# A selective scan with a feed-forward layer on one core: C·h in two runs of four, and side work in six slots a half

## The chip, the cores and the metric

One core of a Trainium2 chip runs the whole program. The metric is the device time of one execution in microseconds. TensorE (PE) multiplies matrices into PSUM, which has eight banks here, all of them in use; ScalarE (ACT) and VectorE (DVE) read PSUM, GpSimd (POOL) works on SBUF alone, and SyncE (SP) issues the DMAs. Each engine runs its own instructions in the order in which the program emits them, and waits on semaphores for the others. The order is written by hand (`tc.manual_schedule()`): what the Python loop emits first stands first in each engine's queue.

## The reference

Two sequences of 1024 tokens with 512 channels go through a selective state-space layer, a residual and a layer norm, then a gated feed-forward layer (512 to 2048 and back), a residual and a layer norm. All values are fp32. The part that sets the shape of the kernel is the recurrence, with 128 states for each of 512 channels:

```python
def step(h, inp):
    dt, bt, ct, xt = inp
    h = jnp.exp(dt[:, :, None] * A) * h + (dt * xt)[:, :, None] * bt[:, None, :]
    y = jnp.einsum('bdn,bn->bd', h, ct)
    return (h, y)
```

`delta`, `B` and `C` come from projections of the normed and gated input; after the scan come `(y + x * D_param) @ out_proj_w.T` and `silu(x @ w_gate.T) * (x @ w_up.T) @ w_down.T`.

## The kernel before

**Rounds.** The 2048 tokens are 64 blocks (`st`) of 32 tokens. A block has two halves (`h`), a half eight rounds, so there are 1024 rounds `k`, and `r = k % 8` is the place of a round in its half. Each round scans 32 channels x 32 tokens for 128 states, as one row of 1024 elements. It emits, in this order:

- `work.others()`: one step of each piece of side work that is at a point marked "E" (ScalarE, GpSimd, VectorE or DMA work, among it what reads the bank of a finished side group).
- TensorE: two `bu` matmuls (L705, outer product of dt·x and B for this round, double-buffered banks), and two `a` matmuls (L417, dt·A of the **next** round). In the trace each fp32 matmul is two records, so a round has eight. The two `a` results have one bank each, so the next round's `a` can be written only when ScalarE has read this round's.
- ScalarE: in odd rounds of every block but the first of a sequence, L713 copies the state carried from the block before into the first column of `bu`; it stands ahead of the two `decay_exp` activations of the next round (L424, `a_sb`). In even rounds VectorE adds it (L723).
- VectorE: the scan (L726), which reads `a_sb` and `bu` and writes `h`.
- TensorE: the `y_round`s that `ROUNDS[r]` lists (L436, C·h of the half before, four matmuls for four tokens; eight `y_round`s a half), or up to four **parts** of side work.
- GpSimd: one `diag` (L388 or L398), which builds an operand for later `bu` or `a` matmuls.

**Side work.** The projections of the next tokens (`pre`), the output projection of finished tokens (`post`) and the feed-forward layer (`ffn`) are generators. They mark "P" before the first matmul of a group, "H" inside a group and "E" after its end. A part is what is emitted between two marks: two `gu` matmuls (L552), one `d` matmul (L574), one `op`, `sel` or `xp` matmul, two transposes. All side groups share one PSUM bank (`misc`, one buffer). A `gu`, `d` or `op` group has eight parts, `sel`, `xp` and `ss` four, the transposes two, `t0` one. `Work.tensor()` emits one part; once a group has ended it emits nothing more until the next `others()` has stepped the generator over its "E". So at most one group ends in a round, and its bank is read in the round after: by ScalarE (L560 for `gu`, L244, L256, L274/L275, L291, L314, L224/L228 for `pre`), or by VectorE (L580 for `d`, L474 for `zT`, L487 for `op`).

**How much a round takes** is set by a credit: each round adds `PARTS[r]`, the sum is cut to 6, and up to `min(credit, 4)` parts are emitted where `PARTS[r]` is not zero.

```python
ROUNDS = ((), (0, 1, 2), (), (), (3, 4, 5), (), (), (6, 7))
PARTS = (4, 0, 3, 3, 0, 3, 3, 0)
```

Both orders give 16 parts of credit a half, which is 128 for four blocks. The work for four blocks is 98 parts of `ffn`, 10 of `post` and some 19 of `pre`.

**After the loop** come the last eight `y_round`s, the last `post` and whatever side work is left, now with six banks and nothing between the groups.

Of the kernel before, what the change touches and what calls it, by code (L numbers as in the profile page):

```python
# [17 lines left out]
TC = 256  # L18


ROUNDS = ((), (0, 1, 2), (), (), (3, 4, 5), (), (), (6, 7))
PARTS = (4, 0, 3, 3, 0, 3, 3, 0)
RMS_EPS = 1e-6
LN_EPS = 1e-5

# [9 lines left out]
def kernel(  # L35
# [26 lines left out]
    NM = D // P  # L62
    NH = NF // 2
# [91 lines left out]

    made = {}

    def misc(name):
        return bank_pool[0].tile([P, 512], FP, tag="m", name=name)


# [3 lines left out]
    def pre(c):  # L165

        t0, n = lots[c]
        n_j, n_s = n // P, n // S
# [29 lines left out]
        for m in range(NM):  # L198
            nc.scalar.activation(xT[:, m, :], xT[:, m, :], AF.Copy, scale=col(V_NORM, m))
        yield "P"  # L200
        ps = misc(f"ss_{c}")
        for k in range(NM):
            nc.tensor.matmul(  # L203
                ps[:, 0:n], ones, u[:, k, :], start=(k == 0), stop=(k == NM - 1)
# [14 lines left out]


        for m in range(NM):
            ps = misc(f"sel_{c}_{m}")
            yield from matmuls(ps, sel_w, m, xn)
            nc.scalar.activation(  # L224
                u[:, m, :], ps[:, 0:n], AF.Relu,
                bias=neg[:, 1, m : m + 1], scale=neg[:, 0, m : m + 1],
            )
            nc.scalar.activation(  # L228
                dt[:, m, :], ps[:, 0:n], AF.Abs, bias=gate_b[:, m : m + 1], scale=col(V_GATE, m)
            )  # L230
            yield "P" if m + 1 < NM else "E"
# [7 lines left out]


        for g, dst in ((0, low), (2, c_sb)):
            ps = misc(f"xp_{c}_{g}")
            yield from matmuls(ps, xp_w, g, xn)
            nc.scalar.copy(dst, ps[:, 0:n])  # L244
            yield "P"

        ps = misc(f"b_{c}")
        for j in range(n_j):
            for k in range(NM):
                nc.tensor.matmul(  # L250
# [12 lines left out]
        yield "P"  # L263

        for a in range(0, NM, 2):
            ps = misc(f"z_{c}_{a}")
            for m in (a, a + 1):
                nc.tensor.matmul(  # L268
                    ps[:, ts(m - a, n)], dt_w[:, ts(m, P)], low, start=True, stop=True
                )  # L270
                yield "H" if m == a else "E"
            for m in (a, a + 1):
                z = ps[:, ts(m - a, n)]
                nc.scalar.activation(u[:, m, :], z, AF.Relu, bias=col(V_DTB, m))  # L274
                nc.scalar.activation(dt[:, m, :], z, AF.Abs, bias=col(V_DTB, m))  # L275
            yield "P" if a == 0 else "E"
# [4 lines left out]

        for j in range(n_j):
            yield "P"
            ps = misc(f"uT_{c}_{j}")
            for m in range(NM):
                nc.tensor.transpose(ps[:, ts(m, P)], u[:, m, ts(j, P)], ident)
                if m == 1:
                    yield "H"
            yield "E"
            t = pre_pool.tile([P, D], FP, tag="row", name=f"uT_{c}_{j}")  # L290
            nc.scalar.copy(  # L291
                t.rearrange("p (g m c) -> p m g c", g=4, m=NM),
                ps.rearrange("p (m g c) -> p m g c", m=NM, g=4),
            )
            for st in range(4):
                nc.sync.dma_start(  # L296
                    ub_d[t0 // S + 4 * j + st, :, :, 0, :].rearrange("g t q -> t g q"),
                    t[ts(st, S), :].rearrange("t (g q) -> t g q", g=4),
                )
            if c == 0:  # L300
                load(0)
                diag(0, 0)
                diag(0, 1)
        yield "P"
        ps = misc(f"t0_{c}")
        for m in range(NM):
            nc.tensor.matmul(
                ps[0:n_s, ts(m, P)],
# [149 lines left out]
    def post(tt):  # L458

        zT = post_pool.tile([P, NM, P], FP, tag="zT", name=f"zT_{tt}")  # L460
        nc.sync.dma_start(zT, x_q.rearrange("(m p) t -> p m t", p=P)[:, :, ts(tt, P)])
        yield "E"
        yield "E"
        nc.gpsimd.tensor_tensor(zT, zT, dq.unsqueeze(2).to_broadcast([P, NM, P]), ALU.mult)
        yield "E"
        yield "P"
        ps = misc(f"zT_{tt}")
        for s in range(4):
            nc.tensor.transpose(ps[:, ts(s, P)], yrs[tt][:, s, :], ident)
            if s == 1:  # L470
                yield "H"
        yield "E"
        z = zT.rearrange("p m (s t) -> p s m t", t=S)
        nc.vector.tensor_tensor(  # L474
            z, z, ps.rearrange("p (s m t) -> p s m t", m=NM, t=S), ALU.add
        )
        x1 = post_pool.tile([P, D], FP, tag="x1", name=f"x1_{tt}", bufs=4)
        nc.sync.dma_start(x1, xf[tt])
        yield "P"
        ps = misc(f"op_{tt}")  # L480
        for half in (slice(0, 256), slice(256, 512)):
            for k in range(NM):
                nc.tensor.matmul(  # L483
                    ps[:, half], zT[:, k, :], out_w[:, k, half], start=(k == 0), stop=(k == NM - 1)
                )
                yield "H" if half.start == 0 or k + 1 < NM else "E"
        nc.vector.tensor_tensor(x1, x1, ps, ALU.add)  # L487
        yield "E"
        yield from normalize(x1, f"a{tt}")
        work.add(ffn(tt, x1))  # L490

    def normalize(t, name):
# [10 lines left out]
    def ffn(tt, row):  # L503
# [4 lines left out]
        for what in order:  # L508
            part = int(what[1])
# [17 lines left out]
        fetch(4)  # L527
        x1T = ffn_pool.tile([P, NM, P], FP, tag="x1T", name=f"x1T_{tt}")
        yield "P"
        ps = misc(f"x1T_{tt}")  # L530
        for m in range(NM):
            nc.tensor.transpose(ps[:, ts(m, P)], row[:, ts(m, P)], ident)
            if m == 1:
# [4 lines left out]
        for what in order:  # L538
            part = int(what[1])
            if what[0] == "g":  # L540
                hid = hid_pool[0].tile([P, NH, P], FP, tag="hid", name=f"hid_{tt}_{part}")
                hids[part] = hid, []

                for f in range(0, NH, 2):
                    fetch(at + 4)
                    yield "P"
                    ps = misc(f"gu_{tt}_{part}_{f}")
                    for b in range(2):
                        w = pieces[at + b].rearrange("p (a k h) -> p a k h", a=2, k=NM)
                        for a in range(2):  # L550
                            for k in range(NM):
                                nc.tensor.matmul(  # L552
                                    ps[:, ts(2 * a + b, P)], w[:, a, k, :], x1T[:, k, :],
                                    start=(k == 0), stop=(k == NM - 1),
                                )
                                if k % 2:
                                    yield "E" if a and b and k + 1 == NM else "H"
                    at += 2
                    gu = ffn_pool.tile([P, 2, 2 * P], FP, tag="gu", name=f"gu_{tt}_{part}_{f}", bufs=2)
                    nc.scalar.copy(gu, ps.rearrange("p (a t) -> p a t", a=2))  # L560
                    work.add(
                        silu(gu, hid[:, f : f + 2, :], f"{tt}_{part}_{f}", hids[part][1]), front=True
                    )
                continue
            hid, ready = hids[part]
            while len(ready) < NH // 2:
                yield "E"
            for half in range(2):
                fetch(at + 4)
                yield "P"  # L570
                ps = misc(f"d_{tt}_{part}_{half}")
                for f in range(NH):
                    w = pieces[at + f // 4].rearrange("p (f d) -> p f d", f=4)
                    nc.tensor.matmul(  # L574
                        ps[:, 0:HD], hid[:, f, :], w[:, f % 4, :],
                        start=(f == 0), stop=(f == NH - 1),
                    )
                    yield "H" if f + 1 < NH else "E"
                part_of = row[:, ts(half, HD)]
                nc.vector.tensor_tensor(part_of, part_of, ps[:, 0:HD], ALU.add)  # L580
                at += 2
# [38 lines left out]
    class Work:  # L620


        def __init__(self):
            self.gens, self.holder = [], None

        def add(self, gen, front=False):
            item = [gen, next(gen)]
# [16 lines left out]
        def tensor(self):  # L644

            if self.holder is not None:
                if self.holder[1] != "H":
                    return False
                self.step(self.holder)
                return True  # L650
            for item in self.gens:
                if item[1] == "P":
                    self.holder = item
                    self.step(item)
                    return True
            return False

# [5 lines left out]
    work = Work()  # L663
# [16 lines left out]
    pres, begun, credit = {}, set(), 0  # L680
    for k in range(NG):
        h, m, pair = place(k)
        st, i = divmod(h, 2)
        r = k % 8
        work.others()
        if r == 0:
# [4 lines left out]
            if i == 0:  # L691
                c = lot_of[st]
# [10 lines left out]
        for b in range(2):  # L703
            g = 2 * pair + b
# [28 lines left out]
            for b in ROUNDS[r]:  # L733
                y_round(h - 1, b)
        credit = min(credit + PARTS[r], 6)
        for _ in range(min(credit, 4) if PARTS[r] else 0):
            if not work.tensor():
                break
            credit -= 1

        j, r4 = divmod(k, 4)
        if r4 == 3:
# [92 lines left out]
```

## Time and profile before

| what | us |
|---|---|
| median of three runs (2877.61 to 2884.94) | 2881.35 |
| the profiled execution's own time | 2885.05 |
| its span, first to last instruction | 2882.4 |
| of the span: lead-in, up to the first round's first `bu` | 40.2 |
| the 1024 rounds (first `bu` of the first to first `bu` of the last) | 2752.0 |
| the last round and what follows the loop | 90.2 |

The stretches are read off the timeline of TensorE. A row of the timeline is: start, duration, engine, line, operation, output<-inputs, count, and in brackets the idle time of the engine before it with what ended it. In the waits, the numbers are total, times and longest. PE rows overlap: their ends are modelled, so a round is best measured from the start of its first `bu` to the start of the next round's.

### The profile page before, as it was taken

To read this page: it belongs to the slowest core of one execution; us is meant where nothing else is said; L and a number is where in the kernel's file an instruction comes from. 1 tells how busy PE (TensorE), PEld (TensorE's weight loads), DVE (VectorE), ACT (ScalarE), POOL (GpSimd) and SP (SyncE) were. 2 spreads that over 40 slices of the span, in tenths; PEclk is the share of its full clock that TensorE was granted. 3 is DMA by queue.
4 is the path that set the end of the run, shared out by engine and by line. 5 is a ranking of instruction groups with operands and counts; after the bars stand their busy time and mean duration, and the time that the engine had idled before them with its cause. 6 is when DMAs were issued, how large, how long until landed. Compare 5 with 4: busy or idle time off the path is not lost.

```text
span 2882.4 us, 58142 instructions
## 1 busy us (share of the span) xinstructions
PE 2781.4 (96%) x22728; PEld 1518.3 (53%) x22728; DVE 2460.8 (85%) x1680; ACT 1640.0 (57%) x3663; POOL 1838.5 (64%) x2140
## 2 busy tenths in 40 slices
PE   7989899999999999999999999999999999999998
PEld 4434454555555555455555555555555555555558
DVE  3998789899998988898998988889998899889970
ACT  4656556555665556555666556655566555555543
POOL 4666576666666666666666666566666666666643
PEclk6999999999999999999999999999999999999999
DMA  2012221324223231223312332222331332333337
GB/s 75 20 34 74 88 89 63 96 73 136 82 76 105 89 122 52 85 96 103 105 56 82 114 103 100 67 91 83 118 100 55 111 100 96 112 102 107 103 107 234
DMA packets 139166, 266.86 MB, mean 93 GB/s; under 512 B 22480, under 2 KB 76240, under 8 KB 138896
## 3 DMA queue, kind: packets, MB, share of 16 engines
q1 hardware_dynamic: 138896, 263.16, 28.5%
q8 instruction: 182, 2.98, 0.4%
q14 instruction: 88, 0.72, 0.1%
HBM read 250.39 MB, written 12.71 MB: 91 GB/s over the span
## 4 chain that ended last, share of the span: by engine, by line
PE 84%; DVE 7%; issue 3%; ACT 3%; POOL 1%; DMA 1%; SPq 0%; DVEq 0%; ACTq 0%; POOLq 0%
PE bu L705 30%; PE gu L552 17%; PE y L436 15%; PE d L574 7%; PE a L417 7%; DVE h L726 6%; PE sel L186 2%; PE op L483 2%; PE xp L186 1%; ACT a_sb L424 1%; DMA ub_d<-uT 1%; PE b L250 1%; PE ss L203 0%; PE z L268 0%; SPq L296 0%
## 5 line engine op out<-in xcount | busy, mean ns | idle before, releaser
L726 DVE TENSOR_TENSOR_SCAN h<-a_sb,bu 128x1024 f32<-128x1024 f32 x1024 | 2326.7, 2283 | 267.1 <-ACT bu L713 144.4
L424 ACT ACTIVATE a_sb<-a 128x496 f32<-128x496 f32 x2048 | 1084.8, 582 | 445.5 <-PE a L417 370.1
L417 PE MATMUL a<-ddt,a_t 32*128 32x512 f32 x4096 | 1275.7, 647 | 7.5 <-ACT a_sb L424 4.7
L705 PE MATMUL bu<-du,ub 32*128 32x512 f32 x4096 | 1224.8, 646 | 28.1 <-DVE h L726 22.7
L388 POOL TENSOR_TENSOR ddt<-dt,hot 128x512 f32<-128x512 f32 x512 | 532.8, 1048 | 291.5 <-PE a L417 291.5
L552 PEld LDWEIGHTS gu<-x1T,w 128*128 128x128 f32 x4096 | 481.9, 192 | 231.1 <-issue 175.2
L398 POOL TENSOR_TENSOR du<-ub,hot 128x512 f32<-128x512 f32 x512 | 534.8, 1048 | 38.9 <-PE a L417 35.2
L552 PE MATMUL gu<-x1T,w 128*128 128x128 f32 x4096 | 536.8, 283 | 11.0 <-ACT x1T L536 3.5
L705 PEld LDWEIGHTS bu<-du,ub 32*128 32x128 f32 x4096 | 351.5, 184 | 354.3 <-issue 209.5
L436 PE MATMUL y<-h,cz 128*32 128x256 f32 x8192 | 523.3, 384 | 1.2 <-DVE h L726 1.2
L436 PEld LDWEIGHTS y<-h,cz 128*32 128x32 f32 x8192 | 227.3, 109 | 403.2 <-issue 291.0
L713 ACT COPY bu<-cu 128x32 f32<-128x32 f32 x496 | 94.1, 190 | 578.0 <-PE a L417 514.5
L417 PEld LDWEIGHTS a<-ddt,a_t 32*128 32x128 f32 x4096 | 393.0, 185 | 47.7 <-ACT a_sb L424 28.8
L592 POOL TENSOR_SCALAR gu<-gu 128x256 f32<-128x256 f32 x128 | 108.2, 845 | 294.0 <-ACT gu L560 289.6
L574 PE MATMUL d<-w,hid 128*128 128x256 f32 x1024 | 257.1, 393 | 7.9 <-ACT t L314 3.0
L574 PEld LDWEIGHTS d<-w,hid 128*128 128x128 f32 x1024 | 184.2, 190 | 126.9 <-issue 81.6
L450 POOL TENSOR_TENSOR yc<-yc,pick 128x512 f32<-128x512 f32 x64 | 66.5, 1039 | 153.7 <-ACT yc L449 153.7
L723 DVE TENSOR_TENSOR bu<-bu,cd 128x32 f32<-128x32 f32 x496 | 92.9, 187 | 74.0 <-PE a L417 69.1
L600 POOL TENSOR_TENSOR hid<-gu,e 128x256 f32<-128x256 f32 x128 | 93.1, 728 | 65.5 <-ACT e L598 64.7
L374 POOL TENSOR_TENSOR cd<-cd,h 128x256 f32<-128x256 f32 x124 | 106.3, 857 | 39.9 <-DVE h L726 39.9
L560 ACT COPY gu<-gu 128x512 f32<-128x512 f32 x128 | 75.0, 586 | 60.3 <-PE gu L552 60.1
L593 POOL TENSOR_TENSOR gu<-gu 128x256 f32<-128x256 f32 x128 | 94.2, 736 | 10.7
(89 smaller groups left out, 1384.0 us busy)
## 6 DMA issues: line engine op xcount, KB each, us to landing
w<-in_wgu_s_dram SPq DMA_DIRECT2D x256, 512.0 KB, 4.8
w<-in_wd_s_dram SPq DMA_DIRECT2D x128, 512.0 KB, 3.8
cd<-dt_d SPq DMA_DIRECT2D x62, 256.0 KB, 3.4
ub<-ub_d SPq DMA_DIRECT2D x64, 128.0 KB, 2.0
cu<-ub_d SPq DMA_DIRECT2D x124, 64.0 KB, 4.8
ub_d<-bt SPq DMA_DIRECT2D x64, 64.0 KB, 1.7
ub_d<-uT SPq DMA_DIRECT2D x64, 64.0 KB, 1.8
zT<-in_x_q_dram SPq DMA_DIRECT2D x16, 256.0 KB
```

The lines of the kernel that those rows point to most:

```text
L374: nc.gpsimd.tensor_tensor(cd, cd, last, ALU.mult)
L388: nc.gpsimd.tensor_tensor(ddts[j][:, m, :, :], made[lot_of[st]][0][:, a + m, toks(st)].unsqueeze(1).to_broadcast([P, 16, S]), hot[:, ts(i, ...
L398: nc.gpsimd.tensor_tensor(dus[j][:, m, :, :], uv[:, a + m, :].unsqueeze(2).to_broadcast([P, 16, S]), hot.unsqueeze(1).to_broadcast([P, 16, ...
L417: nc.tensor.matmul(ps, a_t[ts(g, 32), m, :], ddts[k // 4][ts(g, 32), m % 2, :, :], start=True, stop=True,)
L424: nc.scalar.activation(a_sb[:, k % 3, ts(b, 16), 1:], ps[:, :, 1:], AF.Exp, scale=-1.0)
L436: nc.tensor.matmul(ys[st][ts(m, 32), ts(i, 256)], cz[st % 3][:, at : at + 32], hs[h][:, ts(m, 64), ts(b, 4)], start=(i == 0 and b == 0), s ...
L552: nc.tensor.matmul(ps[:, ts(2 * a + b, P)], w[:, a, k, :], x1T[:, k, :], start=(k == 0), stop=(k == NM - 1),)
L574: nc.tensor.matmul(ps[:, 0:HD], hid[:, f, :], w[:, f % 4, :], start=(f == 0), stop=(f == NH - 1),)
L592: nc.gpsimd.tensor_scalar_max(g, g, -80.0)
L593: nc.gpsimd.tensor_tensor(gu[:, 1, :], g, gu[:, 1, :], ALU.mult)
L705: nc.tensor.matmul(bu[:, ts(b, 16), :], prepared[st][ts(g, 32), 1, :], dus[k // 4][ts(g, 32), m % 2, :, :], start=True, stop=True,)
L726: nc.vector.tensor_tensor_scan(hs[h][:, ts(r, 32), :].rearrange("p q t -> p (q t)"), a_sb[:, k % 3, :, :].rearrange("p q t -> p (q t)"), b ...
```

## The change

The eight `y_round`s of a half go into two rounds (four in `r = 1`, four in `r = 5`) instead of three, and the parts into six rounds instead of five: 3, 2, 3, 3, 2, 3 in `r = 0, 2, 3, 4, 6, 7` (before 4, 3, 3, 3, 3 in `r = 0, 2, 3, 5, 6`). Each side group now tells `Work` how many parts it has, and the loop uses that for its last parts: a group with one part left is finished beyond the credit (up to four parts a round), and a round with three parts emitted and two left in the group stops. The instructions are the same in kind and number; their order changes.

```diff
-ROUNDS = ((), (0, 1, 2), (), (), (3, 4, 5), (), (), (6, 7))
-PARTS = (4, 0, 3, 3, 0, 3, 3, 0)
+ROUNDS = ((), (0, 1, 2, 3), (), (), (), (4, 5, 6, 7), (), ())
+PARTS = (3, 0, 2, 3, 3, 0, 2, 3)
...
-    def misc(name):
+    def misc(name, parts):
+        work.left = parts
         return bank_pool[0].tile([P, 512], FP, tag="m", name=name)
...
-                    ps = misc(f"gu_{tt}_{part}_{f}")
+                    ps = misc(f"gu_{tt}_{part}_{f}", 8)
...
-                ps = misc(f"d_{tt}_{part}_{half}")
+                ps = misc(f"d_{tt}_{part}_{half}", NH)
...
             if self.holder is not None:
                 if self.holder[1] != "H":
                     return False
+                self.left -= 1
                 self.step(self.holder)
                 return True
             for item in self.gens:
                 if item[1] == "P":
                     self.holder = item
                     self.step(item)
+                    self.left -= 1
                     return True
             return False
...
         credit = min(credit + PARTS[r], 6)
-        for _ in range(min(credit, 4) if PARTS[r] else 0):
+        done, most = 0, min(credit, 4)
+        while PARTS[r] and (done < most or done < 4 and work.left == 1):
+
+            if done == 3 and work.left == 2:
+                break
             if not work.tensor():
                 break
-            credit -= 1
+            done += 1
+        credit -= done
```

The other calls of `misc` get the sizes named above (`ss`, `sel`, `xp`: 4; `b`: one or two; `z`, `uT`, `zT`, `x1T`: 2; `t0`: 1; `op`: 8).

More of the change, by code (lines that the diff above doesn't have):

```diff
@@ L200, in pre @@
         yield "P"
-        ps = misc(f"ss_{c}")
+        ps = misc(f"ss_{c}", NM)
         for k in range(NM):
@@ L221, in pre @@
         for m in range(NM):
-            ps = misc(f"sel_{c}_{m}")
+            ps = misc(f"sel_{c}_{m}", NM)
             yield from matmuls(ps, sel_w, m, xn)
@@ L241, in pre @@
         for g, dst in ((0, low), (2, c_sb)):
-            ps = misc(f"xp_{c}_{g}")
+            ps = misc(f"xp_{c}_{g}", NM)
             yield from matmuls(ps, xp_w, g, xn)
@@ L245, in pre @@
             yield "P"
-        ps = misc(f"b_{c}")
+        ps = misc(f"b_{c}", n_j)
         for j in range(n_j):
@@ L265, in pre @@
         for a in range(0, NM, 2):
-            ps = misc(f"z_{c}_{a}")
+            ps = misc(f"z_{c}_{a}", 2)
             for m in (a, a + 1):
@@ L283, in pre @@
             yield "P"
-            ps = misc(f"uT_{c}_{j}")
+            ps = misc(f"uT_{c}_{j}", 2)
             for m in range(NM):
@@ L304, in pre @@
         yield "P"
-        ps = misc(f"t0_{c}")
+        ps = misc(f"t0_{c}", 1)
         for m in range(NM):
@@ L466, in post @@
         yield "P"
-        ps = misc(f"zT_{tt}")
+        ps = misc(f"zT_{tt}", 2)
         for s in range(4):
@@ L479, in post @@
         yield "P"
-        ps = misc(f"op_{tt}")
+        ps = misc(f"op_{tt}", 8)
         for half in (slice(0, 256), slice(256, 512)):
@@ L529, in ffn @@
         yield "P"
-        ps = misc(f"x1T_{tt}")
+        ps = misc(f"x1T_{tt}", 2)
         for m in range(NM):
@@ L623, in __init__ @@
         def __init__(self):
-            self.gens, self.holder = [], None
+            self.gens, self.holder, self.left = [], None, 0
         def add(self, gen, front=False):
```

## The prediction

> **What bounds the kernel now.** I read the page first: which engine the chain lies on, and the clock.
>
> ```profile
> span 2882.4 us, 58142 instructions
> ...
> PE 2781.4 (96%) x22728; PEld 1518.3 (53%) x22728; DVE 2460.8 (85%) x1680; ACT 1640.0 (57%) x3663; POOL 1838.5 (64%) x2140
> ...
> PEclk6999999999999999999999999999999999999999
> ...
> PE 84%; DVE 7%; issue 3%; ACT 3%; POOL 1%; DMA 1%; SPq 0%; DVEq 0%; ACTq 0%; POOLq 0%
> ```
>
> TensorE carries the chain at full clock. But 96% busy hides stalls, since PE rows overlap. So, second, the PE timeline of half a `gu` phase (rounds `r` = 5, 6, 7, 0):
>
> ```profile
> 977.43 0.69 PE L705 MATMUL bu<-du,ub 32*128 32x512 f32 x1
> ...
> 978.50 1.60 PE L552 MATMUL gu<-x1T,w 128*128 128x128 f32 x12
> 980.04 0.69 PE L705 MATMUL bu<-du,ub 32*128 32x512 f32 x1
> ...
> 981.11 0.71 PE L552 MATMUL gu<-x1T,w 128*128 128x128 f32 x4
> 981.75 0.69 PE L705 MATMUL bu<-du,ub 32*128 32x512 f32 x1
> ...
> 983.40 1.07 PE L436 MATMUL y<-h,cz 128*32 128x256 f32 x16
> 984.40 0.69 PE L705 MATMUL bu<-du,ub 32*128 32x512 f32 x1
> ```
>
> A round is measured from its first `bu` to the next. Three parts (12 records): 980.04 - 977.43 = 2.61. One part: 1.71. Undisturbed, the side group starts 1.07 after `bu`; in the round at 981.75 it starts 1.65 after it. That 0.58 is a stall inside the core matmuls, and the busy row doesn't show it. Over all rounds the medians are: 1, 2, 3, 4 parts of `gu` 1.71, 2.16, 2.61, 3.05 (`d`: 3.00 for four); two and three `y_round`s 2.07 and 2.50. So a part costs 0.44, a `y_round` 0.43, and opening a group 0.27 (parts) or 0.21 (`y`) above a bare 1.0. Summed over the timeline, starts later than 1.07 make 181 us.
>
> Third, what the stall waits for, in ScalarE's timeline:
>
> ```profile
> 983.14 0.19 ACT L713 COPY bu<-cu 128x32 f32<-128x32 f32 x1 [0.36 <-PE bu L705]
> 983.26 1.06 ACT L424 ACTIVATE a_sb<-a 128x496 f32<-128x496 f32 x2
> ```
>
> In an undisturbed round the two exps begin 1.24 after `bu` (even rounds) or behind L713 (odd), and end 2.26 or 2.46 after it. The next round's `a` matmuls wait for their banks. So a round shorter than 2.46 (odd) or 2.26 (even) makes the next one stall for the difference: 0.38 after two `y_round`s in `r = 7`, 0.75 after an odd one-part round. VectorE's floor is 4.67 for two rounds, back to back.
>
> Fourth, the waits for the shared side bank where VectorE drains it, and the stretch behind the loop:
>
> ```profile
> PEld d L574 <- DVE x L580: 10.0, 10, 1.4
> ...
> PEld op L483 <- DVE zT L474: 13.9, 11, 1.6
> ```
>
> ```profile
> 2795.93 3.64 PE L436 MATMUL y<-h,cz 128*32 128x256 f32 x58 [1.18 <-DVE h L726]
> 2799.50 3.72 PE L574 MATMUL d<-w,hid 128*128 128x256 f32 x16
> ...
> 2833.51 28.85 PE L552 MATMUL gu<-x1T,w 128*128 128x128 f32 x256 [2.06 <-ACT x1T L536]
> ...
> 2862.20 13.98 PE L574 MATMUL d<-w,hid 128*128 128x256 f32 x64
> ```
>
> Some 37 us behind the last scan finish tile 14 and compute the last attention output; only then does tile 15 start.
>
> **One half by hand.** All `gu`, credit 0 at the start. Before, the credit gives 4, y3, 3, 1 (the group ends, two credits stay over), y3, 4, 4, y2: 3.05 + 2.50 + 2.61 + 1.71 + 2.50 + 3.05 + 3.05 + 2.07 = 20.54, and stalls of 0.75 (behind `r = 3`) and 0.38 (behind `r = 7`): 21.67. The rounds' mean half is 2752 / 128 = 21.5. After: 3, y4, 2, 3, 3, y4, 2, 3. A y4 isn't in the trace; by 0.43 a `y_round` it is 2.93. Sum 20.62. Only the two-part rounds, even ones, are too short: 2 x 0.11. Together 20.84, or 0.83 less.
>
> **The whole loop** is not all `gu`, so I carried the credit rule through all 1024 rounds for both orders, counting the parts of each round and where groups end:
>
> | | before | after |
> |---|---|---|
> | parts left after the loop | 164 | 110 |
> | rounds of 1 / 2 / 3 / 4 parts | 74 / 82 / 99 / 333 | 19 / 297 / 190 / 186 |
> | rounds with no side matmul | 55 | 78 |
> | groups drained by VectorE with the next group in the very next round | 34 | 47 |
>
> - *More parts in the loop.* Credit was lost at the cap and at group ends. 54 x 0.44 = +24. Openings: 127 fewer for `y` (0.21), 104 more for parts (0.27): +1.
> - *Short rounds.* y2 goes: its stalls sum to 37 us. One-part rounds fall by 55, at some 0.4 each: -22. Two-part rounds rise by 215; most cost 0.11, with slower drains among them some 0.12: +26. Odd rounds of three `y_round`s (12 us of stalls before) become y4 with 0.47 to spare, but odd three-part rounds in `r` = 3 and 7 have 0.14: even, +3. Together -30.
> - *Empty rounds.* The work is taken faster and runs dry more often: 23 more rounds that last 1.0 + 1.25 of stall behind them; the 1.25 is new: +29. (The bare 1.0 is in every round.)
> - *Drains one round apart.* L580, L474 and L487 stand behind that round's scan on VectorE, which ends some 3.8 after `bu`; 0.4 to 0.7 of drain follow, and the next group would start 3.7 to 4.1 after it. The waits above price one at 1.0 to 1.3, of which 0.76 is the weight loader's ordinary gap: 0.24 to 0.5. In the worst case, behind a two-part round, 1.35. Thirteen more: +3 to +18; I take 8. While PE waits, the next `bu` and `a` are queued behind that matmul, then the exps and the scan.
> - *The lot boundary.* Rounds 111 and 112 take 13.2 and 4.4, because `finish` must push out the rest of `pre` before the second 256 tokens. By the count `pre` is done by then in the new order: -10.
> - *DMAs and other queues.* The `w` fetches and the stores of `uT`, `bt` and `t` move with their groups on SP. The one `row` buffer makes ScalarE wait for stores ("ACT uT L291 <- DMA ub_d<-uT", 14.3 in four waits) where two `uT` groups and `t0` lie in neighbouring rounds; two or three lots do so in either order. From -8 to +8; I take 0. GpSimd's order changes little: `diag` stays at one a round, with slack 36%.
>
> Sum for the loop: +25 - 30 + 29 + 8 - 10 = +22 if nothing overlaps. But an empty or short round only costs where the rounds around it have not left ScalarE and VectorE behind; going through the rounds in order with these same durations (PE, exps, scan, drains), the stalls of the old order come to 188 (trace: 181), and those of the new one to 17 less instead of 7 more. That takes 24 off: loop -2.
>
> **Behind the loop.** By the count two `d` parts of tile 14 remain instead of 56 parts. From the last scan's end (2795.9): `y` to `yr` 6.6; transposes and `op` 5.7 (as 2802.8 to 2808.2); add and norm 3.5; transposes and copy 2.6; `gu` 28.7; `d` 14.0; last norm and store 6.2: 67.3 against 86.5, -19. The lead-in stays.
>
> **A rule against it.** In that chain PE stands idle about 3.5 us twice (behind the last `y_round`s and behind `op`), where `d` and `gu` of tile 14 filled in before. The clock row shows 9 throughout and 6 only in its first slice: no such gap is in this trace. The Trainium skill ("TensorE: Matmul & The Clock Gate", section "What's actually happening") says that the array falls to half clock after an idle window of about 3.4 us, and needs about as long of work to come back. By the row nothing is lost; by the rule half of 3.4 us twice, 3.4 (an estimate from that page). I take 2: gaps of just this length.
>
> Total: -2 - 19 + 2 = -19. Since a few ScalarE collisions (silu, norms) aren't in the count, I take -17. The profiled execution (2885.05, span 2882.4) lies 3.7 above the median; the difference is carried over to the median: 2881.35 - 17 = 2864.
>
> **The rivals.**
> - *The even half holds everywhere* (few empty rounds cost anything, since the DVE pair floor 4.67 lies under every pair of new rounds: 2.61 + 2.93, 2.16 + 2.61). For it: the `gu` half. Against: 78 empty rounds. About half of 0.83 x 128 = 106 saved, 53, less 24 for the added parts, and the tail's 17: -46, 2835. Chance 0.14.
> - *A wash.* The parts moved into the loop cost what the tail gains, and empty rounds and drains eat the smoothing: loop +17, tail -17: 2881. For it: the sum by single terms gives just that (+22). Chance 0.24.
> - *Slower: ScalarE becomes the bound of the odd three-part rounds.* L713 stands ahead of the exps there, so `r` = 3 and 7 have 2.61 against 2.46. Before, such rounds had four parts or sat beside a `y3`. With groups ending in `r` = 3 and 7, drains (0.59), silu (0.42 + 0.51) and the `yc` copy (0.58) fall into the rounds behind. Where these together pass the free 1.24, the exps slip. It decides from a slip of 0.2 us beyond the slack in one round of each half (26 us); at 0.2 in two rounds it is 51: 2915. Against it: odd y3 rounds had only 0.04 to spare and lost 0.10 on average. Chance 0.14.
> - *Doesn't do what it says*: if waiting on "E" steps stops groups before the credit does, the slots stay short. The count has this in it.
>
> **The numbers.** My forecast has 0.48. Its own range is 2848 to 2878. Low end from the even half, 2834 with rounding; high end 2900 between the wash and the ScalarE case, which leaves out about 0.1 on that side. 0.3% (8.6 us, about what a measurement of this kernel can tell from no change; the three runs span 7.3) puts the borders at 2872.7 and 2890. Faster 0.60: the even half, and most of the forecast. Same 0.24: the wash, and the forecast's upper end, less the wash's own ends. Slower 0.16.
>
> **What would show it.** In the profile after: `y` groups of 32 records with 2.9 from `bu` to `bu`; `gu` groups of 12, 8 and 12; no 0.38 behind `r = 7`; the last `bu` at about 2790 and a tail near 71, with tile 14's weights fetched inside the loop; no pile of `uT` and `t` matmuls near 330 us. It is wrong if the tail is as long as before (the count fails), if side groups start over 1.2 after `bu` in most rounds behind `r` = 3 or 7 (ScalarE), or if L574's waits for L580 grow beyond 30 us (drains).

## The result: 1.1% slower, and the profile after

The changed kernel takes 2912.73 us (median of four, 2908.91 to 2915.46) against 2881.2 of the kernel before (four runs): ratio 1.0108, 95% interval 1.0089 to 1.0128. The forecast was 2864, which is 0.6% faster.

| stretch, us | before | forecast | after |
|---|---|---|---|
| lead-in | 40.2 | same | 40.5 |
| 1024 rounds | 2752.0 | -2 | 2799.6 (+47.6) |
| last round and what follows | 90.2 | -17 | 73.4 (-16.8) |
| span | 2882.4 | 2865 | 2913.5 |

The tail came out as worked out; the whole miss, 50 us (47.6 more instead of 2 less), lies in the loop. The page after, first: totals, clock and chain.

```profile
span 2913.5 us, 58135 instructions
...
PE 2814.4 (97%) x22728; PEld 1541.5 (53%) x22728; DVE 2459.7 (84%) x1680; ACT 1640.5 (56%) x3663; POOL 1837.0 (63%) x2140
...
PE 84%; DVE 6%; issue 3%; ACT 3%; POOL 3%; DMA 1%; SPq 0%; DVEq 0%; ACTq 0%; POOLq 0%
PE bu L709 30%; PE gu L553 18%; PE y L437 15%; PE d L575 8%; PE a L418 7%; DVE h L730 5%; PE sel L187 2%; PE op L484 2%; PE xp L187 1%; ACT a_sb L425 1%; POOL cd L362 1%; DMA ub_d<-uT 1%; PE b L251 1%; POOL du L399 1%; PE ss L204 0%
```

Each engine has as many instructions as before, and ScalarE, GpSimd and VectorE are busy for the same time. PE shows 33 us more for the same 22728 records, which is no more work: its rows stretch where the clock is low and where they wait inside. GpSimd's share of the chain rose from 1% to 3%, with `cd` (L362) and `du` (L399). In the list of waits the first line below is the one that answers:

```profile
ACT cd L363 <- POOL cd L362: 37.9, 24, 2.0
...
PEld d L575 <- DVE x L581: 9.8, 12, 0.9
```

`cd` is the state carried to the next block. `carry_a` (which the diff doesn't touch) is emitted at the end of `r = 5` of a block's first half: a scaling on ScalarE (L361), a product on GpSimd (L362), an exp on ScalarE (L363). Before, this exp (L362 there) waited far less:

```profile
ACT cd L362 <- POOL cd L361: 7.2, 13, 1.1
```

Of the 24 waits after, 16 (30.4 us) come right behind a `gu` group that ended in `r = 4`; the other eight sum to 7.5 us, about what there was before. The bank drains that the prediction worried about (L575 for L581) are no longer than before (10.0).

One such place in the timeline: rounds 357 to 360, the first `bu` of each at 1010.76, 1013.70, 1015.86 and 1020.53. ScalarE and GpSimd:

```profile
1010.87 0.58 ACT L561 COPY gu<-gu 128x512 f32<-128x512 f32 x1 [0.46 <-PE gu L553]
...
1011.54 0.85 POOL L593 TENSOR_SCALAR gu<-gu 128x256 f32<-128x256 f32 x1 [2.73 <-ACT gu L561]
...
1012.47 0.74 POOL L594 TENSOR_TENSOR gu<-gu 128x256 f32<-128x256 f32 x1
...
1013.17 1.05 POOL L399 TENSOR_TENSOR du<-ub,hot 128x512 f32<-128x512 f32 x1
...
1014.18 1.27 POOL L362 TENSOR_TENSOR cd<-a_n,cd 128x512 f32<-128x512 f32 x1
...
1015.48 0.63 ACT L363 ACTIVATE cd<-cd 128x512 f32<-128x512 f32 x1 [1.89 <-POOL cd L362]
1016.01 0.40 ACT L596 ACTIVATE e<-gu 128x256 f32<-128x256 f32 x1
1016.45 0.51 ACT L597 ACTIVATE e<-e,ones 128x256 f32<-128x256 f32 x1
1016.86 1.04 ACT L425 ACTIVATE a_sb<-a 128x496 f32<-128x496 f32 x2
```

Read it as a queue. A `gu` group ended in `r = 4`, so its drain comes in `r = 5`, and its two silu products (L593, L594) stand ahead of `du` and `carry_a`'s product on GpSimd. L363 therefore waits 1.89 us at the head of ScalarE's queue. Behind it stand two silu steps and then the exps of `r = 6` (L425), which were ready some 2 us earlier. In `r = 7` the `a` matmuls need the banks that these exps read: that round's side group starts 3.1 us after its `bu` instead of 1.07. The stall sums (side matmuls that start later than 1.07 after their `bu`) by place in a half show where this happens:

| stalls by `r`, us | 0 | 1 | 2 | 3 | 4 | 5 | 6 | 7 | sum |
|---|---|---|---|---|---|---|---|---|---|
| before | 37 | 14 | 2 | 26 | 19 | 15 | 43 | 25 | 181 |
| after | 23 | 24 | 2 | 27 | 26 | 23 | 4 | 63 | 192 |

`carry_a` belongs to first halves alone, and most of the change in `r = 7` lies there: 45 us of the 63 (before 15). In e1 below, which takes the wait out, 12 are left there, while second halves keep the 18 that they have after.

The second loss is the clock. The trace's record of the granted clock has five stretches at half in the loop before (behind 80 us; 31 us in all), sixteen after (75 us). Both orders also have a long one at the start, from 30 us to 71 after and to 74 before. The other runs agree: the mean granted clock of the span is 0.976 to 0.980 in all four after, and 0.984 to 0.988 in the 88 runs of the kernel before that were taken beside the experiments. The worst places have both:

```profile
1015.86:1020.53 4.67, 4.08 (x21) 2.33 (x20) 3.24 (x2) 3.96 (x10) 2.38 (x4) 1.00 0.00 0
614.80:623.52 8.72, 7.21 (x20) 3.72 (x17) 4.77 (x3) 4.34 (x10) 5.32 (x8) 0.63 0.01 2
2501.62:2510.60 8.98, 7.11 (x20) 3.58 (x16) 4.78 (x3) 4.34 (x10) 5.75 (x8) 0.67 0.00 0
```

These are windows of single rounds with `r = 7`: length, busy time of PE, PEld, DVE, ACT, POOL, then the granted clock. The first has the wait alone and lasts 4.7 us; in the other two an empty round stands ahead, the clock falls to half, and a round at this place, with four `d` parts where the first has three of `gu` (0.4 longer by themselves), lasts 8.7 and 9.0.

### The profile page after: what moved, and what is told of

Its sections match the earlier page's. It is cut to its first block, busy times and chain, and to the rows that moved or that the text cites. A ratio compares the mean times of both kernels' runs of the same rounds, so it can differ in the third digit from the quotient of the medians.

```text
span 2913.5 us, 58135 instructions
## 1 busy us (share of the span) xinstructions
PE 2814.4 (97%) x22728; PEld 1541.5 (53%) x22728; DVE 2459.7 (84%) x1680; ACT 1640.5 (56%) x3663; POOL 1837.0 (63%) x2140
## 4 chain that ended last, share of the span: by engine, by line
PE 84%; DVE 6%; issue 3%; ACT 3%; POOL 3%; DMA 1%; SPq 0%; DVEq 0%; ACTq 0%; POOLq 0%
PE bu L709 30%; PE gu L553 18%; PE y L437 15%; PE d L575 8%; PE a L418 7%; DVE h L730 5%; PE sel L187 2%; PE op L484 2%; PE xp L187 1%; ACT a_sb L425 1%; POOL cd L362 1%; DMA ub_d<-uT 1%; PE b L251 1%; POOL du L399 1%; PE ss L204 0%
## 5 line engine op out<-in xcount | busy, mean ns | idle before, releaser
L425 ACT ACTIVATE a_sb<-a 128x496 f32<-128x496 f32 x2048 | 1084.1, 582 | 590.5 <-PE a L418 545.2
L709 PE MATMUL bu<-du,ub 32*128 32x512 f32 x4096 | 1248.1, 650 | 20.7 <-DVE h L730 18.7
L553 PE MATMUL gu<-x1T,w 128*128 128x128 f32 x4096 | 551.8, 285 | 12.7 <-ACT t L315 5.1
L399 POOL TENSOR_TENSOR du<-ub,hot 128x512 f32<-128x512 f32 x512 | 534.5, 1048 | 17.8 <-PE a L418 12.7
L437 PE MATMUL y<-h,cz 128*32 128x256 f32 x8192 | 502.0, 386 | 0.6 <-DVE h L730 0.6
L437 PEld LDWEIGHTS y<-h,cz 128*32 128x32 f32 x8192 | 242.5, 110 | 334.4 <-issue 203.5
L717 ACT COPY bu<-cu 128x32 f32<-128x32 f32 x496 | 94.6, 191 | 451.0 <-PE a L418 249.7
L593 POOL TENSOR_SCALAR gu<-gu 128x256 f32<-128x256 f32 x128 | 108.2, 846 | 312.8 <-ACT gu L561 310.3
L575 PE MATMUL d<-w,hid 128*128 128x256 f32 x1024 | 268.0, 401 | 2.5 <-ACT t L315 2.3
L575 PEld LDWEIGHTS d<-w,hid 128*128 128x128 f32 x1024 | 185.2, 193 | 145.0 <-issue 94.1
L594 POOL TENSOR_TENSOR gu<-gu 128x256 f32<-128x256 f32 x128 | 94.4, 737 | 10.7
```

Source lines behind the costliest of these rows:

```text
L399: nc.gpsimd.tensor_tensor(dus[j][:, m, :, :], uv[:, a + m, :].unsqueeze(2).to_broadcast([P, 16, S]), hot.unsqueeze(1).to_broadcast([P, 16, ...
L425: nc.scalar.activation(a_sb[:, k % 3, ts(b, 16), 1:], ps[:, :, 1:], AF.Exp, scale=-1.0)
L437: nc.tensor.matmul(ys[st][ts(m, 32), ts(i, 256)], cz[st % 3][:, at : at + 32], hs[h][:, ts(m, 64), ts(b, 4)], start=(i == 0 and b == 0), s ...
L553: nc.tensor.matmul(ps[:, ts(2 * a + b, P)], w[:, a, k, :], x1T[:, k, :], start=(k == 0), stop=(k == NM - 1),)
L575: nc.tensor.matmul(ps[:, 0:HD], hid[:, f, :], w[:, f % 4, :], start=(f == 0), stop=(f == NH - 1),)
L593: nc.gpsimd.tensor_scalar_max(g, g, -80.0)
```

## The experiments

Theory A: in `r = 5` silu's products push `carry_a`'s product back on GpSimd, and the exp that waits for it blocks ScalarE. Theory B: empty rounds let the clock fall, whatever ScalarE does. Theory C: ScalarE's copy L717 ahead of the exps makes odd three-part rounds the bound (the prediction's slower rival). All ratios are to the kernel before on the same chip, with 95% intervals.

**e1 and e2: carry_a's exp two rounds later, in the new and in the old order**

```diff
         nc.gpsimd.tensor_tensor(cd, a_n, cd, ALU.mult)
+
+    def carry_b(st):
+        if st % NSB == 0:
+            return
+        cd, _, _ = carried[st]
         nc.scalar.activation(cd, cd, AF.Exp, scale=-1.0)
...
         if r == 5 and i == 0 and st + 1 < NS:
             carry_a(st + 1)
+        if r == 7 and i == 0 and st + 1 < NS:
+            carry_b(st + 1)
```

> The new order with the second step of carry_a (the exp of cd on ScalarE, L363) emitted two rounds later, at the end of r = 7 of a block's first half instead of r = 5; the GpSimd product before it stays. Theory A (in r = 5 a gu group that ended in r = 4 puts its two silu products, 0.85 and 0.74 us, ahead of carry_a's product on GpSimd; the exp then holds ScalarE's queue for up to 2 us, and with it the exps that the next round's a matmuls wait for): the 38 us of waits of L363 fall to under 5, the stalls of r = 7 fall from 63 to about 30, half-clock windows get fewer, total 2912 to about 2875. Theory B (the loss is the clock that drops where rounds are empty, whatever ScalarE does): 2900 to 2912. Theory C (ScalarE's copy L717 in odd three-part rounds): unchanged, 2905 to 2915.

> The old order with the same step two rounds later. Theory A: no gu group ends in r = 4 of a first half there, and L362's waits are only 7 us, so little: 2872 to 2882. If the move itself is a gain for any order (a shorter ScalarE queue at r = 6), 2860 or less, and then e1 says less about the new order. Theories B and C: 2881.

e1: 2880.23, ratio 0.9989 (0.998 to 0.9997): the loss is gone, 33 us less than after. The stalls of `r = 7` fall from 63 to 30 us, and the waits of the exp no longer appear in the list. e2: 2881.42, ratio 0.9992 (0.9983 to 1.0001): in the old order the same edit does nothing that can be measured. Theory A holds. But e1 is still 16 us short of the forecast, and has 58 us at half clock.

**e3 and e4: the rule for group ends and the order, each alone**

```diff
 e3, to after.py
-ROUNDS = ((), (0, 1, 2, 3), (), (), (), (4, 5, 6, 7), (), ())
-PARTS = (3, 0, 2, 3, 3, 0, 2, 3)
+ROUNDS = ((), (0, 1, 2), (), (), (3, 4, 5), (), (), (6, 7))
+PARTS = (4, 0, 3, 3, 0, 3, 3, 0)
 e4, to before.py: the new ROUNDS and PARTS, the old loop over parts
```

> The old places of y_rounds and parts, with the new rule for a group's last parts alone. By the count 124 parts are left after the loop (before 164, after 110), rounds of one part fall from 74 to 8, empty rounds rise from 55 to 61, and 12 gu groups end in r = 5 and none in r = 4 of first halves. Theory A: the loop stays as it is or gains up to 20, the tail falls by 14: 2855 to 2870. Theory B: half-clock windows stay few (6 more empty rounds): about 2870. If the rule itself is the loss: 2895 or more.

> The new places of y_rounds and parts with the old credit loop. By the count 127 parts are left, 88 rounds have one part, 74 are empty, 14 gu groups end in r = 4 of first halves. The one-part rounds stall again. Theory A: as bad as after or worse, 2910 to 2940, with waits of the cd exp of 30 us or more. Theory B: 2905 to 2925. If the rule is the loss: back to about 2880.

e3: 2867.83, ratio 0.9948 (0.993 to 0.9965). The loop takes 2756 us, the tail 73 instead of 90: the rule is the good half of the change, and what it brings here is the tail. e4: 2903.02, ratio 1.0065 (1.0048 to 1.0082), with the exp's waits at 31.4 us and a loop of 2791. So the loss belongs to the order, as theory A says; that after (2912.73) is slower than e4 fits the count, by which the rule brings 17 `gu` groups to an end in `r = 4` of a first half and the old loop 14, but no run separates that from the clock.

**e5: the new order with e1's move and a filler in empty rounds**

```diff
         credit -= done
+        if PARTS[r] and not done and work.holder is None:
+            ps = bank_pool[0].tile([P, 512], FP, tag="m", name=f"pad_{k}")
+            for n in range(3):
+                nc.tensor.matmul(ps[:, 0:256], ones, cz_pad, start=True, stop=True)
```

> e1 (the new order, carry_a's exp two rounds later) plus three matmuls of 256 columns, whose result nothing reads, in each round that should have a side group and finds no work. e1 has 78 empty rounds, and 58 us of its loop lie in half-clock windows against 31 before. Theory B (empty rounds let the clock drop): the windows fall to under 35 us and the time by 8 to 15, to about 2868. If empty rounds are just bound by ScalarE and VectorE and the clock is no matter: the same, 2878 to 2885. If filling delays the next group or the exps: 2890 or more.

2878.88, ratio 0.9988 (0.9982 to 0.9995): the same as e1, though only 3 us of the loop are at half clock (e1: 58) and the stalls fall to 117. The 78 rounds without side work last 206 us together, 67 more than in e1, which is about what the stalls (43 less) and the clock gave back. What did change is the spread: twenty runs of e1 lie between 2872 and 2890, twenty of this between 2877 and 2881.

**e6 and e7: the state of odd rounds copied by VectorE**

```diff
-            nc.scalar.copy(
+            nc.vector.tensor_copy(
                 bu[:, :, 0].rearrange("p (g e) -> p g e", e=16),
```

> The new order with the state of odd rounds copied by VectorE (tensor_copy) instead of ScalarE (L717). Theory C (L717 ahead of the exps makes odd three-part rounds the bound): the stalls behind odd rounds fall, 2880 or less, and by more than the same edit brings to the old order. Theory A (carry_a's exp waits for GpSimd): the waits of L363 stay near 38 us, and the total stays at 2900 to 2915; an odd round's least length falls from 2.46 to 2.26, worth perhaps 10.

> The old order with the same copy on VectorE. The stalls behind r = 7 (two y_rounds, 2.07 long) should fall from 0.38 to 0.19 and those behind odd one-part rounds from 0.75 to 0.55: 20 to 25 us less by that. Against it VectorE has 0.19 more in odd rounds, where its floor for two rounds goes from 4.67 to about 4.95: 2865 to 2890. Theory C: no more change than in e6.

e6: 2924.45, ratio 1.0145 (1.0127 to 1.0162), slower still, with the exp's waits at 41.4 us. Theory C falls: without L717 on ScalarE the new order loses at least as much. e7: 2883.43, ratio 1.0005 (0.9996 to 1.0013). The stalls behind `r = 7` fall from 37 to 23 us as expected, but the time is the same. VectorE's extra 0.18 us in every odd round may take it back, and so may the clock (55 us at half in its trace behind 80 us, before 31); no run tells them apart.

**e8: three y_rounds in the odd round, two in the even one**

```diff
 to e3
-ROUNDS = ((), (0, 1, 2), (), (), (3, 4, 5), (), (), (6, 7))
+ROUNDS = ((), (0, 1, 2), (), (), (3, 4), (), (), (5, 6, 7))
```

> e3 (the old order with the new rule for group ends) with the two y_rounds in the even r = 4 and three in r = 7. By the sums of the prediction a short even round stalls the next one 0.19 instead of 0.38, and three y_rounds in an odd round 0 to 0.1. The stall sum of r = 0 (41 us) goes, 24 us come back behind r = 4: 2845 to 2860, against 2868 of e3. If L717 does not set the least length of an odd round (theory C and the prediction's stall arithmetic both wrong): the same as e3.

2853.45, ratio 0.99 (0.9882 to 0.9917), 14 us below e3. The stalls of `r = 0` fall from 41 to 5 us, those of `r = 5` rise from 12 to 35: the least length of a round (2.46 odd, 2.26 even) fits what the prediction had.

**e9: only GpSimd's product one round earlier**

```diff
+        if r == 4 and i == 0 and st + 1 < NS:
+            carry_0(st + 1)      # cd = a_n * cd on GpSimd
         if r == 5 and i == 0 and st + 1 < NS:
             carry_a(st + 1)      # the two steps on ScalarE
```

> The new order with only GpSimd's part of carry_a (cd = a_n * cd, L362) moved one round up, to the end of r = 4, ahead of the silu products that a group ending in r = 4 brings in r = 5. ScalarE's two steps stay in r = 5. If the wait on GpSimd's queue is what costs (theory A as told): the 38 us of waits of the cd exp go, as in e1, and the time is 2875 to 2885. If e1 gained because ScalarE's exp left the short r = 6 round: 2895 to 2912.

2867.57, ratio 0.9943 (0.9928 to 0.9958), 45 us below after. ScalarE's instructions stand where they stood; only the order on GpSimd differs. The matching place of the timeline:

```profile
1001.76 0.74 POOL L600 TENSOR_TENSOR gu<-gu 128x256 f32<-128x256 f32 x1
1002.37 0.50 ACT L361 ACTIVATE cu<-cu,b 128x256 f32<-128x256 f32 x1
...
1002.77 0.62 ACT L362 ACTIVATE cd<-cd 128x512 f32<-128x512 f32 x1
1003.29 0.40 ACT L602 ACTIVATE e<-gu 128x256 f32<-128x256 f32 x1
1003.73 0.51 ACT L603 ACTIVATE e<-e,ones 128x256 f32<-128x256 f32 x1
1004.19 1.06 ACT L431 ACTIVATE a_sb<-a 128x496 f32<-128x496 f32 x2
```

The exp follows its neighbour at once, and the exps of the round start 1.8 us behind L361, where the after trace has 3.8. The loop takes 2750.6, the tail 71.2: the forecast's own numbers, 2750 and 73. That they meet so closely is in part luck, since the forecast put the clock at nothing. The half-clock time in the loop falls from 75 to 34 us without any filler, so part of it seems to have been a consequence of the wait (e1, with the wait out too, has 58).

**e10, e13, e14: one unread matmul in each empty round**

```diff
-            for n in range(3):
+            for n in range(1):
 e10: to e5. e13: to after, without e1's move. e14: to before.
```

> e5 with one matmul instead of three in each empty round (some 0.7 us instead of 1.6). e5 took the half-clock windows of the loop from 58 to 3 us and the stalls from 160 to 117, but its 76 filled rounds became longer, and the time stayed at 2879. If the clock is worth what 54 us at half speed say (some 15 to 25): 2860 to 2870 here, with few windows left. If the clock is worth nothing: 2878 to 2882. If one matmul is too little to hold the clock: windows above 30 us, and 2875 to 2880.

> The new order as it is, with one unread matmul in each empty round, and carry_a untouched. Its loop has 75 us at half clock, and 38 us of waits of the cd exp. Clock as a cause of its own: windows under 25 us and 2875 to 2890. Clock only as a consequence of the exp's wait: the wait of 1.9 us leaves TensorE idle all the same, windows above 40 us, 2895 to 2912.

> The old order with the same filler in its 55 empty rounds. It has 31 us of half-clock windows, most of them where ScalarE waits for a DMA at the end of a lot, which a filler does not reach: 2870 to 2882. If it gains as much as e10 did over e1 (22 us), empty rounds cost the same in either order, and the filler says nothing on the new one.

e10: 2857.62, ratio 0.9909 (0.9894 to 0.9924). e13: 2892.18, ratio 1.0033 (1.0025 to 1.0041). e14: 2874.03, ratio 0.9971 (0.9959 to 0.9983). With after and e1 they make a square:

| new order, us | empty rounds empty | one matmul in them |
|---|---|---|
| exp waits for GpSimd | 2912.7, 75 at half clock | 2892.2, 24 at half clock |
| exp two rounds later | 2880.2, 58 at half clock | 2857.6, 10 at half clock |

The half-clock times are those of the loop behind 80 us, from one trace each (e13's was the fastest of its 14 runs). Down a column the wait is worth 33 to 35 us, along a row the clock, less what the matmul itself costs, is worth 21 to 23: they add. In e13 the exp waits as long as in the changed kernel, so the clock is a cause of its own too:

```profile
ACT cd L365 <- POOL cd L364: 38.0, 24, 2.1
```

The old order gains 9 from the same filler: of the clock's cost about 12 us are new, give or take 7 by the intervals. Where the gain lies can be read off the starts of the rounds. The filler also shortens the stretch at half clock at the start, from 41 us to 10 (e13) and from 44 to 17 (e14), and 9 us of e13's gain and 8 of e14's have come by round 24. So most of what the old order gains lies at the start, and what is new lies behind it.

**e11, e12, e15: what the runs point to**

```diff
 e11 = e8 with e1's move;  e12 = e11 with e10's filler;  e15 = e8 with e9's move and the filler
```

> e8 (old places of the parts, group rule, two y_rounds in r = 4 and three in r = 7) with carry_a's exp two rounds later, as in e1. e8 still has 17 us of waits of that exp and 24 us of stalls in r = 6 of first halves: 2838 to 2850 by theory A, 2853 if those waits lie off the path.

> e11 with one unread matmul in each of its 61 rounds that find no work. e8 has only 20 us of half-clock windows, so by the clock theory there is less to win than in e10: 0 to 8 below e11. If it delays: up to 8 above e11.

> e12 with the carry as in e9 (GpSimd's product one round earlier) instead of e1's (the exp two rounds later). e9 was 13 us faster than e1, of which the clock may be the most; with the filler in, 0 to 8 below e12's 2830.5.

e11: 2842.49, ratio 0.9855 (0.9841 to 0.987). e12: 2830.51, ratio 0.9818 (0.9801 to 0.9834), the fastest, 1.8% below the kernel before. e15: 2834.72, ratio 0.9833 (0.9817 to 0.9849): e1's move is the better one in the old places of the parts. There groups do end in `r = 5`, and the exp stands on ScalarE ahead of what reads their bank in `r = 6` (stalls of `r = 6`: 36 us against 27); no run tests that alone. e12 gained 12 from the filler where 0 to 8 were expected. The expectation counted the half clock behind 80 us alone; the stretch at the start fell from 41 us to 24, and 5 us of the gain have come by round 16.

## Why the prediction was wrong

- *What bounds the kernel, and the round arithmetic*: right. A `y4` round lasts 2.94, as from 1010.76 to 1013.70 above (2.93 worked out from 0.43 a `y_round`); its `y` matmuls:

```profile
1011.83 1.94 PE L437 MATMUL y<-h,cz 128*32 128x256 f32 x32
```

  The parts of every round after are those of the count, 78 empty rounds among them.
- *The tail*: right, though its 5.7 for transposes and `op` should read 5.4 by the times given with it. From the last scan's end to the end of the program it is 69.7 us (67.3 plus 2 forecast). The two lines below are `op`, of which the same 16 records took 3.72 before, and the last `gu` run, 28.85 before:

```profile
2852.16 5.41 PE L484 MATMUL op<-out_w,zT 128*128 128x256 f32 x16 [1.39 <-DVE zT L475]
...
2862.86 30.59 PE L553 MATMUL gu<-x1T,w 128*128 128x128 f32 x256 [0.67 <-ACT x1T L537]
```

  The clock record has 10 us at half there. The two rows are 3.4 us longer together, the estimate that the prediction had weighed, where it took 2. *The lot boundary* (-10) was right too: rounds 111 and 112 take 7.8 us, before 17.6.
- *Drains one round apart* (+8): no sign of more. L575 waits for L581 as long as L574 did for L580 (9.8 us, before 10.0).
- *DMAs and other queues* (0): this is the step that failed. It says that GpSimd's order changes little, because `diag` stays at one a round and GpSimd has 36% slack. The slack of an average says nothing on a product that ScalarE waits for in the same round. The change moves the ends of `gu` groups: 17 of 128 end in `r = 4` of a first half after, none before, in the count and in the traces. So it moved silu's products ahead of a step that isn't in the diff, and with it ScalarE's queue. The term was -8 to +8; e1 puts it at 33 us, and e9, with the clock that follows from it, at 45.
- *Empty rounds* (+29) were costed by their stalls alone, and the rule of the clock was weighed for the tail, not for them. The prediction read the row `PEclk` of the page as a clock that never falls in the loop. That row can't show it: 6.8 us at half leave a slice of 72 us at 0.95, still a 9, and the trace before has 31 us at half. With three rounds between two `y` rounds, where before there were two at most, empty rounds stand together: behind round 64 the trace has eight pairs and a three in the new order, one pair in the old, and threes all through the first 64 rounds. e13 and e14 put the clock of empty rounds at 21 us, 12 of them new. That it is their standing together that adds the 12 is argued from the count; no run spreads them.
- *The slower rival* named ScalarE's exps slipping behind `r` = 3 and 7, for L717. They slip behind `r = 6`, and for a wait on GpSimd; without L717 on ScalarE (e6) it is the same. So the sign of the rival was right and its mechanism wrong; that its 2915 lies so near 2912.73 is luck.
- With both losses out (e10), the new order gives 0.9909 of the kernel before; the forecast was 0.994. Against the old order with the same filler (e14) it is 0.994 too.

## What to carry to other kernels

When a schedule moves the ends of groups, list what each end triggers in the rounds behind it, on every in-order queue, and look for steps that another engine waits for at a fixed place, though they aren't in the diff: here a 1.3 us product two places further back held up three engines. Emit a producer on a slow queue a round ahead of its consumer, so that less depends on what comes in between. And where TensorE sets the time, a round without side work can cost twice: its own stall, and the clock of the next 3 to 7 us. One unread matmul in such a round paid here (e10), three did not (e5). To find such stretches, read the clock in short windows, not in the page's forty slices.

## What the runs showed of the hardware

The clock falls without a long idle gap. Two empty rounds (131.32 to 135.40 in the trace after) have no gap over 0.65 us between PE rows, which cover three quarters of the first window below, and the next 3.4 us run at half. (The rows span waiting too, so this share is more than the array worked.)

```profile
131.50:135.90 4.40, 3.38 (x20) 1.57 (x23) 4.30 (x4) 2.23 (x5) 4.10 (x6) 1.00 0.00 0
135.90:139.30 3.40, 3.40 (x16) 1.28 (x13) 3.30 (x3) 1.64 (x3) 2.03 (x2) 0.50 0.00 0
139.30:142.70 3.40, 3.40 (x48) 1.25 (x40) 2.92 (x2) 2.09 (x5) 0.00 (x0) 1.00 0.32 76
```

Behind 80 us, all stretches at half clock in the loop last 3.4, 6.8 or 10.2 us. The Trainium skill ("TensorE: Matmul & The Clock Gate", section "What's actually happening") gives that window, and tells of an idle window before it; here a thinly filled one was enough. A single matmul of 256 columns in each empty round held the clock for the most part: 10 us at half behind 80 us, where e1 has 58 (e10).
